# Seven buffers for the input tiles, and the row transform in four slices between them

## The chip, the cores and the metric

The kernel runs on one core of a Trainium2 chip. The metric is device time in microseconds (us), the median of several runs. The core has a matrix engine (TensorE, PE in the profile; its weight loads are PEld), two elementwise engines (VectorE, DVE, and ScalarE, ACT), a general engine (GpSimd, POOL) and a queue engine (SyncE, SP) that issues transfers. Each engine takes its own instructions strictly in order; they meet at semaphores. Transfers run on 16 DMA engines, whichever engine issued them. SBUF is the on-chip memory of 128 partitions, PSUM the memory that TensorE writes to, HBM the memory outside.

## What is computed

The input `x` has 8 batches of 32 channels of 256 x 256 points. Four layers follow each other, each of them `x + conv(groupnorm(x))`: a spectral convolution, a 5 x 5 convolution, a recurrence along the columns, and a mix of directional maxima. Only the first layer matters here:

```
x_ft   = rfft2(groupnorm(x))
out_lo = einsum('bixy,ioxy->boxy', x_ft[:, :, :32, :32],  w1)   # 32 x 32 lowest modes
out_hi = einsum('bixy,ioxy->boxy', x_ft[:, :, -32:, :32], w2)
x      = x + irfft2(out_ft) + bias
```

Only 64 x 32 of the modes are kept, so the forward transform is two small matrix products: one along the columns of an image (256 points to 32 complex modes), one along its rows (256 points to 64 complex modes). The normalisation is applied to the spectrum afterwards, with the mean and the sum of squares of each pair of channels.

## The kernel before

`forward_and_mix` makes the spectrum and multiplies it by the weights. The later functions (`inverse_and_conv`, `recurrence`, `maxima_and_mix`) are not touched, but the first of them shares SBUF with what is touched.

**Forward transform.** The work goes tile by tile: 8 batches (`b`) of 8 tiles (`n`) of 4 channels, 64 tiles in all. A tile `xa` is 1024 KB (8 KB in each partition), read from HBM by SP (L117). Its pool has four buffers (L103), so the loop keeps three loads ahead of the tile in work (L207, L211). A buffer can be loaded again when its three readers are done: the column matmuls on PE (L132), the squares of half of it on ACT (L141), and the squares of the other half on DVE (L142). The column transform lands in PSUM (`yp`, three buffers), and DVE turns it into `y` (L145). `y` holds a whole batch and has two buffers.

When the eight tiles of a batch are through, the row transform `over_rows` of that batch follows in one piece: 64 matmuls with 32-row operands (L158), two records each in the profile, into four banks of PSUM (`sp`). It stands after the column matmuls of the first tile of the next batch (L217). Right behind it in the same function DVE turns the result into `xb` (L166) and makes two small copies (L171, L172). `statistics` (L179 to L191) comes one tile later, `normalise` two tiles after that (L197, L198): it scales the spectrum, and sends a turned copy of it to `xf` by four transfers that POOL issues (L202).

**Order.** The order on each engine is the order of this code. No planner moves anything in these stages (`manual_schedule`), so what stands behind a waiting instruction on its engine waits too. On DVE the turn L166 stands ahead of the squares L142 of the next tile.

**Weights and mixing.** The weights are eight tiles `wt` of 2048 KB (16 KB in each partition), q = 0 to 7. The first two have buffers of their own in the pool `wp` and are loaded during the last batch, the first of them ahead of the last two input tiles (L212). The other pools of the forward transform are then given up, and a pool `wp2` with four buffers takes their place for q = 2 to 5; its first load (L243, issued at L99) waits until everything of the forward transform is done, the last `xf` transfers included. Tiles 6 and 7 reuse the buffers of 0 and 1 in `wp`. For each q there are 128 matmuls (L258, two records each), copies out of PSUM on ACT (L275) and DVE (L273), and two writes of 256 KB into the HBM tensor `smd` in rows of 128 bytes (L276), one issued by ACT and one by SP.

**What follows.** `inverse_and_conv` reads the spectrum `spec` back from `smd` (L337) and has six buffers for a second copy of the input, `xb<-in_xl_dram`, of 768 KB a load, issued by POOL (L367). These buffers lie in the same part of SBUF as the weight tiles of `wp2`. Their first load waits for the last reader of what was in this part; in the kernel before that is the mixing with q = 5.

Of the kernel before, what the change touches and what calls it, by code (L numbers as in the profile page):

```python
# [9 lines left out]
F32 = mybir.dt.float32  # L10
# [6 lines left out]
P = 128  # L17
B, C, H, W = 8, 32, 256, 256
NG = 16
KM = 32  # L20
# [57 lines left out]
def forward_and_mix(tc, k, d, smd, xmean):  # L78
# [4 lines left out]
    nc = tc.nc  # L83
    CH = 4
    NK = C // CH
    HB = H // 32
    KC = 4
    HW = float(H * W)
    with ExitStack() as ctx:
        one = ctx.enter_context(tc.tile_pool(name="m1", bufs=1))  # L90
        wp = ctx.enter_context(tc.tile_pool(name="mw", bufs=2))


        xf = one.tile([P, 2, B, KM, KM], F32, name="xf")
# [2 lines left out]
        def load_weights(q, wp):  # L97
            wts[q] = wp.tile([P, KM, KC, C], F32, name=f"wt_{q}", tag="wt")
            nc.sync.dma_start(out=wts[q].rearrange("p y j o -> p (y j o)"), in_=d["wm"][q])  # L99

        with ExitStack() as inner:
            fwd = inner.enter_context(tc.tile_pool(name="a1c", bufs=1))
            xp = inner.enter_context(tc.tile_pool(name="a1x", bufs=4))  # L103
            wk = inner.enter_context(tc.tile_pool(name="a1w", bufs=2))
            sm = inner.enter_context(tc.tile_pool(name="a1s", bufs=2))
            ps = inner.enter_context(tc.tile_pool(name="a1p", bufs=1, space=PSUM))
            fh = fwd.tile([P, 2, HB, P], F32, name="fh")
            nc.sync.dma_start(out=fh, in_=d["fh"])
            junk = [fwd.tile([P, 2, 2 * H], F32, name=f"junk_{i}") for i in range(2)]
            units = [(b, n) for b in range(B) for n in range(NK)]  # L110
            zero = fwd.tile([P, B], F32, name="zero")
            xs, ys, squares, turned = {}, {}, {}, {}

            def load(u):
                b, n = units[u]
                xs[u] = xp.tile([P, 2, CH, H], F32, name=f"xa_{u}", tag="xa")
                nc.sync.dma_start(out=xs[u].rearrange("p t c h -> p (t c h)"), in_=d["xt"][b, n])  # L117
# [28 lines left out]
                    ys[b][:, n].rearrange("p r t y -> p (r t y)"), yp.rearrange("p r h -> p (r h)")  # L146
                )

            def over_rows(b):


                sp = ps.tile([P, CH, 512], F32, name=f"sp_{b}", tag="sp")
                y = ys.pop(b)
                for ri in range(2):
                    for t in range(HB):
                        for i in range(CH):
                            r = slice(32 * i, 32 * i + 32)
                            nc.tensor.matmul(  # L158
                                sp[:, i, 0 : NK * KM].rearrange("p (n y) -> p n y", y=KM),
                                lhsT=fh[r, ri, t, :],  # L160
                                rhs=y[r, :, ri, t, :],
                                start=ri == 0 and t == 0,
                                stop=ri == 1 and t == HB - 1,
                            )
                xb = wk.tile([P, KM, KM], F32, name=f"xb_{b}", tag="xb")
                nc.vector.transpose(  # L166
                    xb.rearrange("p y x -> p (y x)"),
                    sp[:, :, 0 : NK * KM].rearrange("p i (n y) -> p y n i", y=KM),
                )
                ex = sm.tile([P, 4, NG, 2], F32, name=f"ex_{b}", tag="ex")  # L170
                nc.vector.tensor_copy(ex, squares.pop(b).unsqueeze(1).unsqueeze(3).to_broadcast([P, 4, NG, 2]))  # L171
                nc.vector.tensor_copy(zero[:, b : b + 1], xb[:, 0, 0:1])  # L172
                turned[b] = xb, ex

            def statistics(b):
# [14 lines left out]
                dc = xb[0:32, 0, 0:1]  # L190
                nc.vector.scalar_tensor_tensor(dc, st[0:32, 0:1], -HW, dc, ALU.mult, ALU.add)  # L191
                turned[b] = xb, rs
# [11 lines left out]
                        )  # L204

            with tc.manual_schedule(engines=None):
                for u in range(3):  # L207
                    load(u)
                for u, (b, n) in enumerate(units):
                    if u + 3 < len(units):  # L210
                        load(u + 3)  # L211
                    if b == B - 1 and n in (2, 5):  # L212
                        load_weights(n // 3, wp)
                    over_columns(u)
                    if b > 0:
                        if n == 0:
                            over_rows(b - 1)  # L217
                        elif n == 1:
                            statistics(b - 1)
                        elif n == 3:  # L220
                            normalise(b - 1)
                over_rows(B - 1)
                statistics(B - 1)
                normalise(B - 1)
                by_group = fwd.tile([P, B, NG], F32, name="by_group")
                nc.vector.tensor_tensor(
                    by_group,
                    k.sel.unsqueeze(1).to_broadcast([P, B, NG]),
                    zero.unsqueeze(2).to_broadcast([P, B, NG]),
                    ALU.mult,  # L230
                )
                xm = ps.tile([P, B, NG], F32, name="xm", tag="st")
                nc.tensor.matmul(xm, lhsT=k.ones, rhs=by_group, start=True, stop=True)
                nc.vector.tensor_copy(xmean, xm)

        wp2 = ctx.enter_context(tc.tile_pool(name="mw2", bufs=4))
        sp = ctx.enter_context(tc.tile_pool(name="ms", bufs=2))
        ps = ctx.enter_context(tc.tile_pool(name="mp", bufs=4, space=PSUM))
        NQ = KM // KC
        KY = KM // 2  # L240
        with tc.manual_schedule(engines=None):
            for q in range(2, 6):
                load_weights(q, wp2)  # L243
            for q in range(NQ):
                if 2 <= q < 4:
                    load_weights(q + 4, wp)
                wt = wts.pop(q)
                mps = [
                    [ps.tile([P, 2 * B, 2, KY], F32, name=f"mp_{q}_{s}_{h}", tag=f"mp{s}") for h in range(2)]
                    for s in range(2)  # L250
                ]


                for ky in range(KM):
                    for j in range(0, KC, 2):
                        for s in range(2):
                            r = slice(64 * s, 64 * s + 64)
                            nc.tensor.matmul(  # L258
                                mps[s][ky // KY][32 * j : 32 * j + 64, :, :, ky % KY],
                                lhsT=wt[r, ky, j : j + 2, :].rearrange("p j o -> p (j o)"),  # L260
                                rhs=xf[r, :, :, ky, KC * q + j : KC * q + j + 2].rearrange("p r b x -> p (r b) x"),
                                start=True,
                                stop=True,
                            )
                for s in range(2):
                    sm = sp.tile([P, B, 2, KM], F32, name=f"sm_{q}_{s}", tag=f"sm{s}")
                    for h in range(2):
                        for j in range(KC):
                            r = slice(32 * j, 32 * j + 32)
                            src = mps[s][h][r, :, j % 2].rearrange("p (r b) y -> p b r y", r=2)  # L270
                            dst = sm[r, :, :, h * KY : (h + 1) * KY]
                            if s:
                                nc.vector.tensor_copy(dst, src)  # L273
                            else:
                                nc.scalar.copy(dst, src)  # L275
                    (nc.scalar, nc.sync)[s].dma_start(  # L276
                        out=smd[:, :, s, KC * q : KC * (q + 1)].rearrange("b r j o y -> (j o) (b r) y"),
                        in_=sm.rearrange("p b r y -> p (b r) y"),
                    )


def inverse_and_conv(tc, k, d, smd, xmean, x2d, stb):
# [8 lines left out]
    QP = Q + 2  # L291
    HW = float(H * W)

# [5 lines left out]
    with ExitStack() as ctx:  # L299
# [26 lines left out]
        def by_pair(t):  # L326
            return t.rearrange("p (k c g) -> p k c g", c=2, g=G)

        def twice(t, n):
            return t.rearrange("p (k g) -> p k g", g=G).unsqueeze(2).to_broadcast([P, n, 2, G])  # L330
# [11 lines left out]
        def spectrum(b):  # L342
# [14 lines left out]
            nc.vector.tensor_tensor(by_pair(up), by_pair(bias), twice(m1, 4), ALU.subtract)  # L357
            nc.vector.scalar_tensor_tensor(t[0:1, :, 0, 0], up[0:1], HW, t[0:1, :, 0, 0], ALU.mult, ALU.add)
            for a in range(A):
# [703 lines left out]
```

## Time and profile before

| | |
|---|---|
| time, median of 3 runs | 3496.8 us (3491.6 to 3498.0) |
| span of the profiled run | 3489.2 us |
| forward transform: first tile in, last tile in | 14.0 us, 251.7 us |
| first matmul of the mixing, last one | 271.3 us, 353.6 us |
| first matmul of the inverse transform (L388) | 372.0 us |

The profile can be read as a page of sums, as tables of busy time by stretch, as a list of who waited for whom, as the chain of work that ended last, or as a list of instructions in order of time. In the tables of stretches each engine has its busy time and its number of instructions (x), and then come the granted TensorE clock (1.00 is full), the share of time in which the DMA engines were busy (it can exceed 1 a little) and the bytes they moved. In a list by time the first two columns are start and duration in us, and the bracket at the end tells how long the engine had been idle and what it had waited for; "issue" is idle time for which no wait is recorded. "SPq" and "ACTq" are the queues of transfers.

The stages of interest are the first 372 us of the 3489 us. The rest is the same code on the same data in both kernels.

### The profile page before, as it was taken

What the parts mean: (1) busy time and instruction counts of PE and PEld (TensorE: products, weight loads), DVE (VectorE), ACT (ScalarE), POOL (GpSimd) and SP (SyncE); (2) the same over time, 40 slices, a digit from 0 to 9 for tenths busy, and PEclk for the clock granted to TensorE, in tenths of its full rate; (3) what the DMA queues carried; (4) which work ended last, traced back from release to release, by engine and by line L of the source; (5) the groups of instructions that cost most, each with busy time, mean ns of one, the idle gap of its engine ahead of it and who ended that gap; (6) DMA issues with size and microseconds to landing.
All of it is one profiled execution on the core that took longest, in us unless ns stands there. A gap on an engine that the chain in (4) does not pass through costs nothing.

```text
span 3489.2 us, 114177 instructions
## 1 busy us (share of the span) xinstructions
PE 3125.8 (90%) x48474; PEld 1700.8 (49%) x48474; DVE 2590.4 (74%) x5178; ACT 1810.0 (52%) x4098; POOL 883.8 (25%) x1211
## 2 busy tenths in 40 slices
PE   6776599999999969999999999999999867777787
PEld 4546244444444446666666666666666523232332
DVE  5553255556555548888888888888888889999998
ACT  3322255655665547777677777776777512222222
POOL 0010011111111025444444444454444400000000
PEclk9985699999999979999999999999999979999898
DMA  8887467777777445555455555545554377777775
GB/s 309 285 293 237 98 179 184 189 184 186 198 173 198 101 125 143 136 134 143 126 131 141 146 124 147 131 129 133 144 126 123 83 286 309 307 301 293 305 306 235
DMA packets 533869, 655.78 MB, mean 188 GB/s; under 512 B 394992, under 2 KB 395888, under 8 KB 507632
## 3 DMA queue, kind: packets, MB, share of 16 engines
q1 hardware_dynamic: 492272, 499.58, 50.9%
q0 software_dynamic: 15360, 79.70, 6.8%
q10 hardware_dynamic: 25728, 69.21, 5.0%
q8 instruction: 381, 6.24, 0.7%
q14 instruction: 128, 1.05, 0.1%
HBM read 371.54 MB, written 272.63 MB: 185 GB/s over the span
## 4 chain that ended last, share of the span: by engine, by line
PE 63%; DVE 22%; issue 4%; DMA 1%; SPq 1%; ACT 1%; POOL 0%; DVEq 0%; ACTq 0%; POOLq 0%
PE r L686 9%; PE r L660 8%; PE vp L446 7%; PE vp L454 7%; PE z L686 6%; PE ni L686 6%; PE z L660 6%; PE ni L660 5%; DVE rv L885 5%; PE up L405 4%; DVE dq L898 2%; DVE uq L899 2%; PE tp L388 2%; PE mp L258 1%; DVE top L896 1%
## 5 line engine op out<-in xcount | busy, mean ns | idle before, releaser
L739 POOL TENSOR_TENSOR xw<-xw,hs 128x256 f32<-128x256 f32 x512 | 349.8, 683 | 661.9 <-DVE hs L738 620.4
L936 ACT ACTIVATE ot<-o,bres 128x512 f32<-128x512 f32 x256 | 155.1, 688 | 551.6 <-PE o L920 545.0
L735 POOL TENSOR_TENSOR a<-zm,xn 128x256 f32<-128x256 f32 x510 | 392.5, 770 | 154.0 <-ACT zm L732 140.2
L728 ACT ACTIVATE rs<-r,brz 128x256 f32<-128x256 f32 x510 | 239.4, 469 | 286.0 <-PE r L660 285.8
L471 ACT ACTIVATE junk<-x 128x128 f32<-128x128 f32 (+1 forms) x384 | 202.8, 528 | 329.6 <-DVE x L465 323.5
L686 PE MATMUL r<-hs,wmain 128*128 128x256 f32 x1020 | 357.4, 432 | 1.9 <-DVE hs L738 1.2
L413 DVE TENSOR_TENSOR x<-up,xb 128x512 f32<-128x512 f32 x288 | 185.5, 686 | 227.6 <-PE up L405 217.6
L660 PE MATMUL r<-xn,whh 32*32 32x256 f32 x4080 | 323.8, 386 | 29.5 <-ACT xn L653 29.5
L729 DVE SCALAR_TENSOR_TENSOR n<-nh,bhh,rs 128x256 f32<-128x256 f32 x510 | 245.7, 482 | 114.0 <-ACT rs L728 114.0
L733 ACT ACTIVATE n<-n,bih 128x256 f32<-128x256 f32 x510 | 259.2, 508 | 132.2 <-DVE n L730 132.2
L660 PE MATMUL r<-hs,wih 32*32 32x256 f32 x4080 | 323.3, 386 | 0.0
L465 DVE SCALAR_TENSOR_TENSOR x<-vp,r,x 128x128 f32<-128x128 f32 (+2 forms) x512 | 236.8, 514 | 110.1 <-PE vp L454 109.9
L660 PE MATMUL ni<-hs,wih 32*32 32x256 f32 x4080 | 311.6, 373 | 2.6 <-issue 2.6
L660 PE MATMUL nh<-xn,whh 32*32 32x256 f32 x4080 | 312.5, 375 | 0.8 <-issue 0.8
L660 PE MATMUL z<-xn,whh 32*32 32x256 f32 x4080 | 311.8, 374 | 0.0
L660 PE MATMUL z<-hs,wih 32*32 32x256 f32 x4080 | 310.9, 373 | 0.3 <-issue 0.3
L686 PE MATMUL z<-hs,wmain 128*128 128x256 f32 x1020 | 303.8, 379 | 0.0
L686 PE MATMUL ni<-hs,wmain 128*128 128x256 f32 x1020 | 303.4, 379 | 0.0
L446 PE MATMUL vp<-x,c_conv 128*128 128x256 f32 (+2 forms) x768 | 290.0, 512 | 2.0 <-DVE x L465 2.0
L763 DVE TENSOR_TENSOR fm<-xw,fm 128x512 f32<-128x512 f32 x255 | 289.7, 1136 | 1.4 <-POOL xw L739 0.8
L920 PE MATMUL o<-dn,wsc 32*32 32x512 f32 x1536 | 208.4, 790 | 78.1 <-DVE dn L901 73.2
L454 PE MATMUL vp<-x,c_conv 64*64 64x256 f32 (+2 forms) x1536 | 277.7, 492 | 0.0
(160 smaller groups left out, 6277.0 us busy)
## 6 DMA issues: line engine op xcount, KB each, us to landing
xb<-in_xl_dram POOLq DMA_DIRECT2D x96, 768.0 KB, 6.0
xa<-in_xt_dram SPq DMA_DIRECT2D x64, 1024.0 KB
xw<-x2d SPq DMA_DIRECT2D x32, 2048.0 KB
x3d<-xw SPq DMA_DIRECT2D x256, 256.0 KB
fwd<-fm SPq DMA_DIRECT2D x256, 256.0 KB
x<-x3d SPq DMA_DIRECT2D x32, 2048.0 KB
fw<-fwd SPq DMA_DIRECT2D x32, 2048.0 KB
out_dram<-ot ACTq DMA_DIRECT2D x64, 1024.0 KB
```

Source lines behind the costliest of these rows:

```text
L446: nc.tensor.matmul(vp, lhsT=k.conv[:, 0:P], rhs=pair_of(u, ch, g, lo, hi), start=True, stop=False)
L454: nc.tensor.matmul(vp[o], lhsT=k.conv[r, P : P + 64], rhs=pair_of(u, ch, g, lo, hi, q0, r), start=False, stop=True,)
L465: nc.vector.scalar_tensor_tensor(x, src, state[u]["r"][ch][:, g : g + 1], x, ALU.mult, ALU.add, accum_out=s1[:, 0, n, ch, g : g + 1])
L660: return nc.tensor.matmul(out[rows(j)], lhsT=lhsT, rhs=rhs[rows(i)], start=start, stop=stop)
L686: nc.tensor.matmul(psums[n, key], lhsT=wmain[:, gate, :], rhs=prev[:, :, 1 : 1 + Q], start=gate == N, stop=False)
L728: nc.scalar.activation(r, p["r"], AF.Sigmoid, bias=brz[:, 0:1])
L729: nc.vector.scalar_tensor_tensor(m, p["nh"], bhh[:, 2:3], r, ALU.add, ALU.mult)
L733: nc.scalar.activation(m, m, AF.Tanh, bias=bih[:, 2:3])
L735: nc.gpsimd.tensor_tensor(a, zm, cur, ALU.mult)
L739: nc.gpsimd.tensor_tensor(raw, raw, new, ALU.add)
L763: ins = nc.vector.tensor_tensor(t[:, :, wi], x, last, ALU.max)
L920: nc.tensor.matmul(pts[b2][i][32 * j : 32 * j + 32].rearrange("p (w q) -> p w q", q=Q), lhsT=wsc[q, b2, t, :], rhs=src[j][q, b2], start=first,
```

## The change

The input tiles get seven buffers instead of four, so that six loads run ahead. The row transform is cut into four slices of 16 matmuls, and one slice each follows the column matmuls of the tiles n = 0 to 3 of the next batch. The turn L166 with its two copies becomes a function of its own and comes after tile n = 4, the statistics after n = 5, the normalisation after n = 7: DVE is to meet a result that is ready. For the last batch, which has no next one, the row transform is done in two halves of columns: the half that belongs to tiles 0 to 3 after the column matmuls of tile 6, the other half after tile 7.

The three more input buffers need 24 KB in each partition. To make room, `wp` keeps one buffer, so only weight tile 0 is loaded during the forward transform (now after all input tiles have been issued), and tile 1 joins those that are loaded afterwards; `wp2` gets five buffers, and tiles 6 and 7 reuse buffers there: tile 6 that of tile 1, tile 7 that of tile 2.

```diff
+    AHEAD = 7
+    SLICES = 4
...
-        wp = ctx.enter_context(tc.tile_pool(name="mw", bufs=2))
+        wp = ctx.enter_context(tc.tile_pool(name="mw", bufs=1))
...
-            xp = inner.enter_context(tc.tile_pool(name="a1x", bufs=4))
+            xp = inner.enter_context(tc.tile_pool(name="a1x", bufs=AHEAD))
...
-            def over_rows(b):
+            def over_rows(b, i, lo=0, hi=NK):
...
+                steps = [(ri, t) for ri in range(2) for t in range(HB)]
+                size = len(steps) // SLICES
+                for ri, t in steps[i * size : (i + 1) * size]:
+                    for c in range(CH):
+                        r = slice(32 * c, 32 * c + 32)
+                        nc.tensor.matmul(
+                            sps[b][:, c, lo * KM : hi * KM].rearrange("p (n y) -> p n y", y=KM),
+                            lhsT=fh[r, ri, t, :],
+                            rhs=ys[b][r, lo:hi, ri, t, :],
...
+            def turn(b):
...
-                for u in range(3):
+                for u in range(AHEAD - 1):
                     load(u)
                 for u, (b, n) in enumerate(units):
-                    if u + 3 < len(units):
-                        load(u + 3)
-                    if b == B - 1 and n in (2, 5):
-                        load_weights(n // 3, wp)
+                    if u + AHEAD - 1 < len(units):
+                        load(u + AHEAD - 1)
+                    if b == B - 1 and n == 2:
+                        load_weights(0, wp)
                     over_columns(u)
                     if b > 0:
-                        if n == 0:
-                            over_rows(b - 1)
-                        elif n == 1:
+                        if n < SLICES:
+                            over_rows(b - 1, n)
+                        elif n == SLICES:
+                            turn(b - 1)
+                        elif n == SLICES + 1:
                             statistics(b - 1)
-                        elif n == 3:
+                        elif n == SLICES + 3:
                             normalise(b - 1)
-                over_rows(B - 1)
+                    if b == B - 1 and n == NK - 2:
+                        for i in range(SLICES):
+                            over_rows(b, i, 0, NK // 2)
+                for i in range(SLICES):
+                    over_rows(B - 1, i, NK // 2, NK)
+                turn(B - 1)
...
-        wp2 = ctx.enter_context(tc.tile_pool(name="mw2", bufs=4))
+        wp2 = ctx.enter_context(tc.tile_pool(name="mw2", bufs=5))
...
-            for q in range(2, 6):
+            for q in range(1, 6):
                 load_weights(q, wp2)
             for q in range(NQ):
                 if 2 <= q < 4:
-                    load_weights(q + 4, wp)
+                    load_weights(q + 4, wp2)
```

## The prediction

> **What bounds the kernel now.** The change touches the first 372 us alone, so I read that part. First the waits of the queue that issues the loads, from 36 to 251 us (us in total, times, longest):
>
> ```profile
> SPq L117 <- DVE junk L142: 150.4, 52, 10.5
> SPq L117 <- PE yp L132: 20.5, 14, 2.4
> ```
>
> The loads of x wait for a buffer, mostly for DVE to finish with the old tile, once as long as 10.5 us. Then the DMA by stretch, around the row transform of batch 0:
>
> ```profile
> 30.00:42.00 12.00, 10.45 (x176) 7.46 (x180) 5.71 (x10) 5.67 (x10) 0.00 (x0) 1.00 1.01 424
> ...
> 43.00:49.00 6.00, 6.00 (x101) 4.03 (x99) 3.72 (x12) 0.95 (x2) 0.00 (x0) 1.00 0.15 37
> 49.00:54.00 5.00, 4.69 (x88) 2.73 (x84) 5.00 (x10) 0.75 (x1) 2.01 (x2) 1.00 0.88 354
> 54.00:64.00 10.00, 4.96 (x86) 2.72 (x76) 6.52 (x12) 4.89 (x9) 1.70 (x4) 1.00 0.98 306
> ```
>
> Undisturbed, the DMA is full at 424 GB/s: a tile of 1.049 MB takes 2.47 us. From 43 to 49 us it is nearly empty (0.15 busy). Why, the lists of DVE and PE by time show:
>
> ```profile
> 36.94 0.72 DVE L145 STREAM_TRANSPOSE y<-yp 128x512 f32<-128x512 f32 x1 [0.66 <-PE yp L132]
> 45.18 1.25 DVE L166 STREAM_TRANSPOSE xb<-sp 128x1024 f32<-128x1024 f32 x1 [7.53 <-PE sp L158]
> ```
>
> ```profile
> 36.81 3.72 PE L158 MATMUL sp<-y,fh 32*128 32x256 f32 x60
> 40.98 4.15 PE L158 MATMUL sp<-y,fh 32*128 32x256 f32 x68 [0.45 <-issue]
> 45.06 1.93 PE L132 MATMUL yp<-xa,c_fw 128*32 128x256 f32 x32
> ```
>
> DVE stands 7.5 us before the turn L166, with the squares of the following tiles behind it. No buffer comes free, the three loads ahead run out, and the DMA stops. So the forward transform is bound by transfers, with a hole of about 6.3 us per batch. Check: 14.0 (first tile in) + 63 x 2.47 + seven times 4.1 (the `xf` transfers, below) + 5 (weight tile 0, ahead of the last two tiles) = 203; the last tile came at 251.7, which leaves 48.4 for seven holes, 6.9 each. It fits.
>
> The end of the stage and the mixing, from the lists by time and the chain that ended last:
>
> ```profile
> 255.83 7.19 PE L158 MATMUL sp<-y,fh 32*128 32x256 f32 x128 [0.83 <-DVE y L145]
> ...
> 272.25 6.92 PE L258 MATMUL mp<-xf,wt 64*64 64x32 f32 x281 [0.58 <-DMA xf<-xb]
> ```
>
> ```profile
> 334.62 0.56 POOL L367 DMA_DIRECT2D xb<-in_xl_dram  x1 [64.88 <-PE mp L258]
> ```
>
> ```profile
> 335.79 18.41 DMA smd<-sm
> ...
> 357.80 2.96 DMA smd<-sm
> ```
>
> From last tile to end of rows is 11.35 us, from there to the mixing 9.2. Near the end of the mixing POOL starts six loads for the next stage, and the `smd` writes, needed two rounds later, take 18.4 us instead of 3. The packets by queue from 342 to 350 us (packets, MB, share) show how (q0 the loads, q1 and q10 `smd`):
>
> ```profile
> q0 software_dynamic: 548, 2.98, 89.8%
> q1 hardware_dynamic: 665, 0.09, 6.8%
> q10 hardware_dynamic: 626, 0.08, 6.4%
> ```
>
> About one small packet per large one: some 83 per us on a queue, where one write has 2048.
>
> **What the Trainium skill says.** "DMA: Bandwidth & Descriptors", section "Queues, rings and completion order": each DMA engine goes round the queues that have work, packet by packet. The counts above agree. "Runtime: NRT & Kernel Launch", "Instruction fetch mechanics": instructions come in blocks of 256, fetched by DMA. The trace agrees: with the DMA full, the mixing matmuls come in groups of 127 or 128 records (with their weight loads 256 instructions) with gaps of 2.4 to 2.6 us; with it empty, gaps of 0.2. "TensorE: Matmul & The Clock Gate", "What's actually happening": after about 3.4 us of idleness the clock is halved. Here a tile's matmuls took 1.93 us, and 3.59 after waits of over 3 us at 66 us. The same page, "LDWEIGHTS (loading the stationary operand)": columns / 1.2 ns, 107 for 128 columns, whatever the rows; no row of before shows it apart.
>
> **The change, part by part.**
>
> *Seven buffers, slices, later turn.* At tile n = 4 the last slice has been done since before that tile's column matmuls, so L166 finds its result; its 1.6 us with the copies delay the next squares by no more, and six loads ahead are 6 x 2.47 = 14.8 us of stock. All holes go. What can take their place, per batch: DMA 8 x 2.47 + 4.1 = 23.9 us. The 4.1: from 54 to 64 us, with the `xf` transfers, queue 1 moved 2.52 MB instead of 4.24. PE: 8 x 1.93 + 7.2 + 0.4 (statistics) = 23.0, in blocks of 128 records of 7.2 us, longer than the 6.2 us in which the full DMA brings a block in the mixing. DVE: 8 x 1.75 (its pitch where it never waits, from 50.13 to 51.88 us) + 1.6 + 0.8 + 0.7 = 17.1. So the DMA stays the bound, at 97% of which PE is busy too. Six of the `xf` groups fall before the last tile (that of batch 6 now comes with tile 63), and weight tile 0 comes after it. Last tile in: 14.0 + 63 x 2.47 + 6 x 4.1 = 194. With so little room PE will fall behind at times; I add 3 us (a choice; bounds 0 and 14, the first rival). 197 instead of 251.7: **-54.7 us**.
>
> *The last batch in halves.* Each half is again 128 records, half as long. By the skill's price four loads of 107 ns on four row groups side by side give 27 ns a record, 3.4 us a half; at today's rate of 56 ns it would be 7.2. The first half delays the last tile's columns, as PE has only 2.5 us between two tiles. Best: 9.5 us after the last tile. With one fetch gap of 2.5 us in each half, as in the mixing under full DMA: up to 14.5. Before: 11.35. I take **0**, with -2 and +3 as ends. The chain from the turn to the mixing (9.2 us) stays; the `xf` transfers of batch 6 lie ahead of it, beside matmuls.
>
> *Weight tile 1 after the stage.* Five loads instead of four stand before the mixing's writes: 2.1 MB, 5 us more of full DMA. Tile 1 is there about 7 us after its issue, when the matmuls of q = 0 end. No matmul waits for it. But for 5 us longer PE runs at 6.2 us a group instead of 3.8: **+2 to +3**.
>
> *The next stage's loads.* Weight tile 7 now lies in `wp2`, where those six buffers will be. In the changed program their first load waits for the matmuls of q = 7, not q = 5. That takes the collision out of the last two rounds: two gaps of 2.4 become 0.2, **-4.4**. But it moves it to the last `smd` writes, on which the reading back of the spectrum waits. Call the last mixing matmul M. Before: last write landed at M + 7.1. After: copies end at M + 2, writes start at M + 2.6; the loads start at M + 2.4 (as at 334.4 to 336.8), and 4.7 MB at 395 GB/s take 12 us. At 83 packets per us, 980 of 2048 pass until M + 14.4, with some 400 more while the loads start up (a guess), and the rest in 1 us: M + 15.4, **+8.3**. If the writes slip through first, M + 5.5 and the readback (8192 small packets) meets the loads instead: about +4.
>
> Mixing and handover: 2.5 - 4.4 + 8.3 = +6.4. Sum: -54.7 + 0 + 6.4 = -48.3, or 3448.5. I say **3449**.
>
> **The rivals.**
> - *PE becomes the bound.* Before, PE was busy 24.4 us per batch, slow clock included; with a fetch gap of 0.4 twice, 25.3. Seven batches at 25.3 after the first put the last tile at 14 + 20 + 177 = 211: 3463. For: PE is within 1 us of the DMA, and idle waits bring the slow clock back. Against: most slow stretches followed the holes.
> - *The handover costs nothing,* the halves save their 2 us and PE keeps up: -57.7 - 2 + 2.5 - 4.4 + 4 = -58, 3439. For: reads and writes of `smd` are short when undisturbed (3 us). Against: the packet counts.
> - *Slower.* The holes are not a matter of buffers: some other wait (ACT or PE) releases the tiles as late as DVE did, and the handover's 6 us stays: 3503. Against: PE is the last to release in only 20.5 us of waits, and the squares on ACT kept pace while DVE stood.
>
> **How the numbers follow.** Main case 0.68, PE-bound 0.15, free handover 0.13, slower 0.04. The range 3435 to 3466 takes in the first three with their bounds. Faster by over 0.2% (7 us) 0.95, within it 0.01, slower 0.04.
>
> **What would show it.** Right: no stretch with an empty DMA between 15 and 195 us, the waits of L117 on DVE short, the last tile at about 197, the mixing starting at about 217, L367 released by the end of the mixing, and a `smd` wait of over 10 us right before the readback. Wrong: PE busy without a break and tiles waiting in their buffers (first rival); the readback starting 3 us after the last `smd` write was issued (second); L117 waiting as before (third).

## The result, and the profile after

| | before | changed |
|---|---|---|
| time, median of 4 runs each | 3494.2 us (3480.9 to 3498.0) | 3443.2 us (3441.8 to 3444.8) |
| ratio, 95% interval | | 0.9861 [0.9833, 0.9888] |
| span of the profiled run | 3489.2 us | 3441.9 us |
| last tile in | 251.7 us | 194.5 us |
| end of the last row transform | 263.0 us | 207.3 us |
| first matmul of the mixing | 271.3 us | 215.7 us |
| end of its last matmul | 353.6 us | 295.3 us |
| readback of the spectrum begins | 360.9 us | 313.6 us |
| first matmul of the inverse transform | 372.0 us | 324.75 us |

The kernel became faster by 51.0 us by the medians. The profiled runs differ by 47.3 us, and the whole of that lies ahead of the inverse transform: its first matmul (L388, now L402) comes 47.26 us earlier. The further working uses these two profiled runs, unless another is named. (The kernel before has one run more here than in its own table above.)

First the waits of the queue that issues the loads (L119, formerly L117), from 36 to 195 us:

```profile
SPq L119 <- DVE junk L144: 80.2, 49, 2.8
SPq L119 <- PE yp L134: 38.1, 25, 1.9
```

The queue still waits often, since it runs far ahead, but its longest wait for DVE is 2.8 us where it was 10.5. That is about the transfer of one tile, and six are in stock. The stretches around the row transform of batch 0, and one in the middle (PE, PEld, DVE, ACT and POOL busy, clock, DMA share, GB/s), show what that does to the transfers:

```profile
30.00:42.00 12.00, 10.90 (x188) 7.16 (x184) 8.19 (x14) 5.51 (x10) 0.00 (x0) 1.00 1.01 419
42.00:54.00 12.00, 11.65 (x203) 6.99 (x196) 6.09 (x13) 5.75 (x10) 0.00 (x0) 1.00 1.01 416
54.00:66.00 12.00, 11.87 (x200) 7.72 (x204) 11.25 (x24) 5.24 (x8) 3.71 (x5) 1.00 1.02 412
108.00:132.00 24.00, 23.52 (x405) 14.94 (x400) 17.52 (x36) 10.83 (x19) 4.05 (x7) 1.00 1.02 385
```

The DMA is full in each of them; the stretch with a share of 0.15 is gone. In the last row another thing is to be seen: PE is busy for 23.52 of 24 us. So two resources are at their limit at once. PE's list by time shows how the slices lie:

```profile
36.64 2.01 PE L161 MATMUL sp<-y,fh 32*128 32x256 f32 x32
38.58 1.93 PE L134 MATMUL yp<-xa,c_fw 128*32 128x256 f32 x32
40.44 2.01 PE L161 MATMUL sp<-y,fh 32*128 32x256 f32 x32
```

A slice of 2.0 us and a tile of 1.93 us take turns, where one block of 7.9 us stood between two tiles before. At the end of the stage:

```profile
195.06 1.93 PE L134 MATMUL yp<-xa,c_fw 128*32 128x256 f32 x32
196.93 3.85 PE L161 MATMUL sp<-y,fh 32*128 32x128 f32 x128
200.71 1.93 PE L134 MATMUL yp<-xa,c_fw 128*32 128x256 f32 x32
203.48 3.85 PE L161 MATMUL sp<-y,fh 32*128 32x128 f32 x128 [0.84 <-DVE y L147]
215.67 0.39 PE L272 MATMUL mp<-xf,wt 64*64 64x32 f32 x2 [2.66 <-DMA xf<-xb]
```

ACT takes up the last tile at 194.53, but only at 195.06 does PE begin with the columns of the tile before it. It is one tile behind when the input ends. The two halves of the row transform take 3.85 us each.

The rest is in the chain of work that ended last, and in POOL's list by time:

```profile
297.07 16.30 DMA smd<-sm
...
316.89 5.99 DMA spec<-smd
```

```profile
295.91 0.56 POOL L381 DMA_DIRECT2D xb<-in_xl_dram  x1 [81.73 <-PE mp L272]
```

The loads of the next stage (L381) are released by the end of the mixing, as the change of pools implies, and the last `smd` writes, begun at about 297, take 16.3 us. Before, a write of 18.4 us lay in the mixing, and the last one took 3.

### The profile page after: what moved, and what is told of

Its sections match the earlier page's. It is cut to its first block, busy times and chain, and to the rows that moved or that the text cites. A ratio compares the mean times of both kernels' runs of the same rounds, so it can differ in the third digit from the quotient of the medians.

```text
span 3441.9 us, 114429 instructions
## 1 busy us (share of the span) xinstructions
PE 3118.1 (91%) x48602; PEld 1690.7 (49%) x48602; DVE 2589.1 (75%) x5178; ACT 1808.5 (53%) x4098; POOL 883.6 (26%) x1211
## 4 chain that ended last, share of the span: by engine, by line
PE 65%; DVE 21%; issue 3%; DMA 2%; SPq 1%; ACT 1%; POOL 0%; DVEq 0%; POOLq 0%; ACTq 0%
PE r L700 9%; PE r L674 8%; PE vp L460 7%; PE vp L468 7%; PE z L700 6%; PE ni L700 6%; PE z L674 6%; PE ni L674 5%; DVE rv L899 5%; PE up L419 4%; DVE dq L912 2%; DVE uq L913 2%; PE tp L402 2%; PE mp L272 1%; DVE top L910 1%
```

## The experiments

Eleven kernels were run. Times are medians of 4 runs (20 for one kernel, which is said there), with the ratio to runs of the kernel before on the same chip; where the text says a single run, there is only the profiled one. "Last tile" is the time at which ACT takes it up.

### Which half of the change does it

**Buffers alone.** Seven buffers and the pools of weights as changed, but the rows in one piece and turned at once, as before:

```diff
-                        if n < SLICES:
-                            over_rows(b - 1, n)
-                        elif n == SLICES:
+                        if n == 0:
+                            for i in range(SLICES):
+                                over_rows(b - 1, i)
                             turn(b - 1)
-                        elif n == SLICES + 1:
+                        elif n == 1:
                             statistics(b - 1)
-                        elif n == SLICES + 3:
+                        elif n == 3:
                             normalise(b - 1)
```

(The last batch's rows are in one piece too.)

> The changed kernel with the row transform in one piece again, at the first tile of the next batch, with its turn right behind it, and whole for the last batch; the seven buffers and the pools of the weights stay. My theory: the hole is a matter of stock. DVE stands some 10 us per batch, six loads ahead are 14.8 us, so the DMA keeps running: last tile in at 195 to 200 (changed kernel: 194.5), time about 3446. Rival: the late turn and the slices do most of it, since the squares wait behind the turn just as long: last tile at 225 or later, time 3470 or more.

Measured: 3443.8 us (3442.8 to 3444.7), ratio 0.9869 [0.9852, 0.9886]; last tile at 197.28, inverse transform at 325.64. The waits of the loads from 36 to 190 us, and one stretch in the middle:

```profile
SPq L119 <- DVE junk L144: 109.9, 49, 9.9
```

```profile
108.00:132.00 24.00, 23.47 (x428) 16.89 (x424) 16.69 (x33) 11.39 (x19) 3.46 (x5) 1.00 1.02 387
```

DVE stands before the turn as long as ever, and a load waits 9.9 us for it, yet the DMA stays full: six loads ahead bridge it. What follows: the stock alone removes the hole. In the changed kernel slices and late turn add nothing that shows in the time (3443.8 against 3443.2, and 3447.1 when the changed kernel was measured again).

**Slices alone.** Slices, late turn and halves, but four buffers and the weights as in the kernel before:

```diff
-    AHEAD = 7
+    AHEAD = 4
...
-        wp = ctx.enter_context(tc.tile_pool(name="mw", bufs=1))
+        wp = ctx.enter_context(tc.tile_pool(name="mw", bufs=2))
...
-        wp2 = ctx.enter_context(tc.tile_pool(name="mw2", bufs=5))
+        wp2 = ctx.enter_context(tc.tile_pool(name="mw2", bufs=4))
```

(with tiles 0 and 1 loaded in the last batch, and 6 and 7 into `wp`, as before)

> The changed kernel with four buffers of x again and the weight pools of before; slices, late turn and halves stay. My theory: without the stock the loads follow PE through tiles 0 to 3 (two pieces of 1.9 us each per tile, 3.75 us) and the DMA through tiles 4 to 7, and the xf transfers add to it: 26 to 28 us per batch, last tile at about 222, time about 3465 with the handover of before. Rival: the slices alone are enough, 25 us per batch: last tile at 214 or earlier, 3457 or less. Other rival: four buffers keep the holes: over 240, 3485.

Measured: 3448.4 us (3444.7 to 3451.1), ratio 0.9885 [0.9864, 0.9906]. One stretch in the middle, and the arrival of the last tile at ACT:

```profile
84.00:108.00 24.00, 23.01 (x392) 14.54 (x388) 15.95 (x33) 10.24 (x17) 3.07 (x5) 1.00 1.02 371
```

```profile
208.90 1.06 ACT L143 ACTIVATE junk<-xa 128x1024 f32<-128x1024 f32 x1 [1.30 <-DMA xa<-in_xt_dram]
```

Three loads ahead are enough too, once no DVE wait is long: the first tiles of batches 3 and 7 come at 87.07 and 184.97, which is 24.5 us per batch, against 23.4 in the changed kernel (shown below). I had expected 26 to 28; the first rival of that expectation came. The last tile comes 14.4 us later than in the changed kernel, 5 us of that because weight tile 0 is loaded ahead of the last two tiles. But the inverse transform starts at 329.89, only 5.1 us later, and the time is 5.2 us longer. Some 9 us come back behind the last tile, where this kernel keeps the old pools and so the old handover. The two halves of the change are two cures of one hole; the second of them needs no memory.

### What bounds the forward transform now

Three kernels, a single run each. The first leaves out half of the row transform's matmuls:

```diff
-                steps = [(ri, t) for ri in range(2) for t in range(HB)]
+                steps = [(ri, t) for ri in range(2) for t in range(HB // 2)]
```

> The changed kernel with half of the row transform's matmuls left out (t below 4 of 8), so that the spectrum is not the right one; all transfers stay. It asks whether PE or the DMA sets the pace of 23 us per batch, with PE busy 98% and the DMA full. DMA the bound (the prediction): the last tile still comes at 194 to 196, PE now waits for tiles, and only the end of the stage gets some 4 us shorter. PE the bound: PE needs 3.6 us less per batch, the last tile comes at 186 or earlier.

The second leaves out the `xf` transfers of all batches but the last, with zeros in their place:

```diff
+        nc.gpsimd.memset(xf[:, 1], 0.0)
...
-                for s in range(2):
+                for s in range(2 if b == B - 1 else 0):
```

> The changed kernel with the turned copies into xf left out for all batches but the last (that half of xf holds zeros, so the spectrum's product is wrong); all matmuls stay. If the DMA alone set the pace, 4.1 us less of transfers per batch would bring the last tile to 175 or so. If PE, which is busy 98%, is as close as it looks, the pace stays at 23 us per batch and the last tile at 192 to 195, with loads waiting for buffers.

The third does both.

> The changed kernel with both left out: half of the row matmuls, and the xf copies of all batches but the last (the result is wrong on both counts). If the two are level bounds, neither alone moves the last tile much and both together do: 2.47 us a tile without a break, the last one at about 170. If one of them was the only bound, this run gives the same as the one that left it out.

The same stretch in the three, in this order, each followed by the arrival of the last tile at ACT:

```profile
108.00:132.00 24.00, 21.14 (x342) 13.07 (x340) 18.07 (x35) 11.17 (x18) 3.46 (x5) 1.00 1.02 386
...
194.41 1.06 ACT L143 ACTIVATE junk<-xa 128x1024 f32<-128x1024 f32 x1 [1.31 <-DMA xa<-in_xt_dram]
```

```profile
108.00:132.00 24.00, 23.52 (x404) 14.92 (x400) 17.52 (x36) 10.24 (x17) 2.05 (x2) 1.00 0.98 355
...
191.44 1.06 ACT L144 ACTIVATE junk<-xa 128x1024 f32<-128x1024 f32 x1 [0.49 <-DMA xa<-in_xt_dram]
```

```profile
108.00:132.00 24.00, 22.84 (x376) 13.23 (x376) 18.76 (x36) 11.53 (x21) 1.46 (x1) 1.00 1.01 419
...
177.21 1.06 ACT L144 ACTIVATE junk<-xa 128x1024 f32<-128x1024 f32 x1 [1.31 <-DMA xa<-in_xt_dram]
```

These marks count from the start of the run, and the first tile does not come at the same time in every run: at 13.88 us in the changed kernel's profile, at 16.00 in a second profile of it (below), at 15.75, 16.35 and 16.17 here. Counted from the first tile, the last one comes after 180.7 and 178.3 us in the changed kernel, and after 178.7, 175.1 and 161.0 us in these three. Less work for PE alone moves it not at all: the DMA holds it, at 386 GB/s. Fewer transfers alone move it by some 3 us: now PE holds it, and the DMA falls to 355 GB/s. Both together bring it 17 us earlier. So neither is the bound alone; they are level. The times were 3439.2, 3443.6 and 3422.5 us, beside 3492.5 for the kernel before.

The pace says the same. PE's list of the changed kernel has the statistics of batch 0 and of batch 6:

```profile
54.08 0.38 PE L186 MATMUL ms<-zero,c_msel 128*128 128x1 f32 x2 [0.43 <-DVE zero L179]
...
194.53 0.38 PE L186 MATMUL ms<-zero,c_msel 128*128 128x1 f32 x2 [0.43 <-DVE zero L179]
```

Six batches in 140.45 us are 23.4 us per batch, with one wait of 0.43 us in each. In the first of the three kernels, where the DMA alone sets the pace, the first tiles of batches 3 and 7 come at 81.07 and 174.44, which is 23.3 us per batch. In the third they come at 81.02 and 162.08: 20.3 us per batch, or 2.53 us a tile. What is left of 23.3 is an estimate for a group of `xf` transfers, 3.1 us. The prediction had 2.47 and 4.1. In the third kernel I had expected the last tile at 170; from 156 to 180 us its PE is busy for 23.52 of 24 us again, so that its last tiles wait for PE.

### The last batch in halves

The changed kernel with the last batch's rows in one piece after the last tile (a single run), and the changed kernel itself once more:

```diff
-                    if b == B - 1 and n == NK - 2:
-                        for i in range(SLICES):
-                            over_rows(b, i, 0, NK // 2)
                 for i in range(SLICES):
-                    over_rows(B - 1, i, NK // 2, NK)
+                    over_rows(B - 1, i)
```

> The changed kernel with the last batch's row transform in one piece after the last tile, not in two halves. By the prediction's step the halves are worth nothing, between 2 us saved and 3 lost: the rows end at 207 in both, the mixing starts at 215 to 217. If the halves save their time: rows end at 209 or later. If the first half held up the last tile: at 205 or earlier.

> The changed kernel itself, beside the others of this call: 3443 again, between 3440 and 3447.

The arrival of the first tile at ACT and the rows on PE, first with the rows in one piece, then in the changed kernel's second profile:

```profile
15.67 1.06 ACT L143 ACTIVATE junk<-xa 128x1024 f32<-128x1024 f32 x1 [13.64 <-DMA xa<-in_xt_dram]
...
202.28 7.19 PE L161 MATMUL sp<-y,fh 32*128 32x256 f32 x128 [1.77 <-DVE y L147]
```

```profile
16.00 1.06 ACT L143 ACTIVATE junk<-xa 128x1024 f32<-128x1024 f32 x1 [13.97 <-DMA xa<-in_xt_dram]
...
205.58 3.85 PE L161 MATMUL sp<-y,fh 32*128 32x128 f32 x128 [0.84 <-DVE y L147]
```

In one piece the rows end at 209.47, in the changed kernel at 207.33 and, in its second profile, at 209.43. These 2.1 us between two profiles of one program are those by which the first tile came later. Counted from the first tile, the rows of the changed kernel end after 193.45 and 193.43 us, and after 193.43 and 193.41 in the first two kernels of the next section, which have the same code up to there. In one piece they end after 193.80. So the halves are worth 0.4 us, which cannot be seen in a time: two halves of 3.85 us are 0.5 us more matmul than one piece of 7.19, and the wait for `y` before them is 0.84 us instead of 1.77. Times: 3444.8 us in one piece, 3447.1 (3444.0 to 3447.8), ratio 0.9872 [0.9858, 0.9887], for the changed kernel again.

### Where the rest of the gain went: the handover

The last tile comes 57.2 us earlier, but the inverse transform 47.3, and the medians gained 51.0 us and, measured again, 43.2. Two kernels try to get the difference back, and two more follow them up.

**The collision back in the mixing.** Weight tile 6 goes into tile 0's buffer, 1 and 7 share a pool of their own outside the part of SBUF that the next stage takes. The loads L381 then wait for the mixing with q = 5 again:

```diff
+        wp1 = ctx.enter_context(tc.tile_pool(name="mw1", bufs=1))
-        wp2 = ctx.enter_context(tc.tile_pool(name="mw2", bufs=5))
+        wp2 = ctx.enter_context(tc.tile_pool(name="mw2", bufs=4))
...
-                load_weights(q, wp2)
+                load_weights(q, wp1 if q == 1 else wp2)
...
-                    load_weights(q + 4, wp2)
+                    load_weights(q + 4, wp if q == 2 else wp1)
```

> The changed kernel with weight tiles 1, 6 and 7 out of the pool wp2: 6 in the buffer of tile 0, 1 and 7 in a pool of one buffer, so that the next stage's first load waits for q = 5 again. If the collision of these loads with the last smd writes costs the handover 11 us: the last write lands about 7 us after the last mixing matmul (changed kernel: 18), the mixing itself gets some 4 us longer, tile 1 comes a little earlier, the inverse transform starts 8 or 9 us earlier: 3434 to 3436. If the writes at the end are slow for another reason: last write still at 15 or more after the last matmul, 3443.

Measured: 3440.5 us (3436.2 to 3447.2), ratio 0.9861 [0.9841, 0.9882], so not the 3434 to 3436 that I had hoped for. Its chain that ended last, and PE at the start of the mixing:

```profile
215.79 8.96 DMA xf<-xb
...
288.69 17.97 DMA smd<-sm
...
310.26 2.95 DMA smd<-sm
```

```profile
219.78 0.39 PE L273 MATMUL mp<-xf,wt 64*64 64x32 f32 x2 [4.67 <-DMA xf<-xb]
```

The last `smd` write is short again, 2.95 us. But the write of 18 us is back in the mixing, which takes 86.6 us from first to last matmul where the changed kernel needs 79.6. And tile 1's load, which no longer waits for the forward transform to end, now runs beside the last `xf` transfers, and they take 8.96 us instead of 2.8. From the last mixing matmul to the inverse transform it is 18.6 us where the changed kernel needs 29.5, so 10.9 are gained, but 6.9 are lost in the mixing, and the mixing begins 2.1 us later, counted from the first tile. The inverse transform starts at 324.89 (changed kernel: 324.75 and, in its second profile, 325.85): the collision was moved, not removed. That tile 1's load makes the `xf` transfers long is read from this one profile; no kernel here takes it away alone.

**The loads after the readback.** The changed kernel, and ahead of the first load of the next stage one copy on POOL of a number of the spectrum into the load's buffer. The load has to follow that copy, and the copy has to follow the readback:

```diff
+                if u == 0 and ch == 0 and i == 0:
+                    nc.gpsimd.tensor_copy(t[:, 0, 0, 0:1], specs[0][:, 0, 0, 0:1])
```

> The changed kernel, with the next stage's loads held back until the spectrum has been read: GpSimd copies one number of it into the first buffer ahead of the first load. If the collision is the cause: last smd write 5 us after the last mixing matmul, readback and preparation 11 us, inverse transform at 312 instead of 324.7, and the loads land well before the first addition that needs them: about 3430. If it is not: 3443. If the loads then come too late for that addition: DVE waits for xb, and part of the 13 us is lost.

Measured: 3431.85 us (3430.1 to 3433.7), ratio 0.9835 [0.9818, 0.9852], faster than both kernels. Its chain, and then the list by time of POOL, PE and DVE:

```profile
298.53 4.21 DMA smd<-sm
...
306.15 6.05 DMA spec<-smd
```

```profile
313.33 3.26 POOL L383 DMA_DIRECT2D xb<-in_xl_dram  x6 [2.92 <-issue]
...
314.13 1.98 PE L404 MATMUL tp<-c_eh,spec 128*64 128x256 f32 x8 [3.33 <-DVE spec L372]
...
336.70 1.29 DVE L429 TENSOR_TENSOR x<-up,xb 128x512 f32<-128x512 f32 x2 [22.25 <-PE up L421]
```

The last write takes 4.2 us instead of 16.3, and the inverse transform starts at 314.13, 10.6 us earlier although the first tile came 2 us later. From the last mixing matmul to there it is 17.4 us instead of 29.5. The loads are issued at 313.33, 17 us later, and nobody misses them: the first that needs `xb`, the addition at 336.70, waits for PE alone. That shows the collision as the cause of the long write, and its price as some 12 us.

**The same edit on the kernel before.**

> The kernel before with one edit: the next stage's loads are held back until the spectrum has been read. If their collision with the smd writes cost the kernel before something too: the gaps of 2.4 us in the last two rounds of the mixing go, the wait of 18.4 us for smd goes, the inverse transform starts at 366 to 367 instead of 372.0: 3488 to 3490 beside 3494. If the collision cost nothing there, because it lay inside the mixing: no change.

Measured: 3487.4 us (20 runs) beside 3490.4 of the kernel before (23 runs), ratio 0.9991 [0.9985, 0.9998]. PE's list by time:

```profile
342.48 6.76 PE L258 MATMUL mp<-xf,wt 64*64 64x32 f32 x240 [0.16 <-issue]
...
366.89 1.98 PE L390 MATMUL tp<-c_eh,spec 128*64 128x256 f32 x8 [3.42 <-DVE spec L358]
```

The mixing takes 77.6 us from first to last matmul instead of 82.3, and the handover after it 17.7 instead of 18.4. So in the kernel before the collision cost 5.5 us between the first matmuls of the mixing and of the inverse transform (3.0 by the medians of the time), in the changed one some 12. The change doubled it. Compared with the loads held back in both, the forward part is worth 366.89 - 314.13 = 52.8 us.

**Five buffers, slices, the old pools of weights, loads held back.** If slices need little stock, five input buffers leave room for both early weight tiles:

```diff
-    AHEAD = 7
+    AHEAD = 5
...
-                    if b == B - 1 and n == 2:
-                        load_weights(0, wp)
+                    if b == B - 1 and n in (4, 5):
+                        load_weights(n - 4, wp)
```

(with `wp` of two buffers, `wp2` of four, and the copy on POOL)

> Slices and late turn with five buffers of x, the weight pools of the kernel before (tiles 0 and 1 loaded early, but both after the last tile of x), and the next stage's loads held back. Four loads ahead are 9.9 us of stock, and four buffers with slices already gave 24.3 us per batch: last tile at 195 to 198, mixing from about 217, with four weight loads instead of five ahead of the writes 2 to 3 us shorter than in the changed kernel, handover 17.5 us: inverse transform at 310 to 312, about 3428. If seven buffers are needed: last tile at 204 or later, 3436.

Measured: 3432.25 us (3424.6 to 3436.4), ratio 0.9829 [0.9812, 0.9847]; last tile at 199.15 (195 to 198 expected), inverse transform at 315.23. It is not better than the kernel with seven buffers and held loads (3431.85). From the first tile to the mixing it takes 204.3 us instead of 201.8, in the mixing 77.4 instead of 79.1: what the early tile 1 may gain, the forward transform loses.

## Why the prediction was right, point by point

The predicted 3449 is 5.8 us above the median; the likeliest case is the one that came, and its sum agrees with the profiled runs within about 1 us, -48.3 against -47.2. That closeness is in part luck: the terms missed by -2.5, +1.6, -0.8 and +2.8 us and cancelled.

| step | predicted | measured |
|---|---|---|
| last tile in | -54.7 | -57.2 |
| from there to the mixing | 0 (-2 to +3) | +1.6 |
| mixing, first to last matmul | +2.5 - 4.4 = -1.9 | -2.7 |
| last mixing matmul to inverse transform | +8.3 | +11.1 |
| sum | -48.3 | -47.2 |

**The forward transform.** The diagnosis held: the waits on DVE and the empty DMA went together, and the last tile came at 194.53, where the working gave 194. The 3 us that I added for PE falling behind did not show at the last tile. They belong to what follows: PE falls behind the tiles, and the end of the rows keeps its distance to the first tile within 0.04 us whether the last tile comes 178 or 181 us after the first. Two sizes in the working were off and cancelled in large part: a tile takes 2.53 us rather than 2.47, a group of `xf` transfers 3.1 rather than 4.1. The cause "DVE stands" was right, but either cure was enough, and the prediction treated them as one.

**"So the DMA stays the bound"** was half right. PE is as near to its limit: removing work from one of them gains some 3 us at most, from both 17. The sign that I had named for the first rival, PE busy without a break, is there but for one wait of 0.43 us per batch, and tiles do wait in their buffers. What the rival had wrong is its price: 25.3 us a batch with slow clock and fetch gaps. Measured were 23.4 us, at full clock. The slow stretches left with the holes: from 140 to 195 us the granted clock (third column from the end) was 0.88 in the kernel before, as the first line shows, and is 1.00 in the changed one, the second.

```profile
140.00:195.00 55.00, 43.03 (x664) 26.85 (x660) 33.04 (x65) 18.59 (x31) 6.92 (x10) 0.88 0.84 303
```

```profile
140.00:195.00 55.00, 53.62 (x908) 33.77 (x900) 38.25 (x74) 23.25 (x39) 6.92 (x10) 1.00 1.01 382
```

**The last batch in halves.** From the last tile to the mixing +1.6 us in the pair of profiles that I compare, but +3.8 in the second profile of the same kernel (194.32 to 217.73), so "0, with -2 and +3" was the right order. The last tile is a poor mark for this step, as PE works from its buffers: from the first tile to the mixing the two profiles agree, 201.8 and 201.7 us. The halves ran at 3.85 us for 128 records, 30 ns each. The Trainium skill, "TensorE: Matmul & The Clock Gate", section "LDWEIGHTS (loading the stationary operand)", had led me to an estimate of 27, and the trace is near it. But that does not show that the weight loads set this pace: half of the 56 ns at 256 columns would be 28. The prediction was wrong to say that no row of the kernel before shows these loads: its profile records them, with 185 ns each as a median where the estimate had 107, and it is 185 to 187 in the changed kernel too. These records overlap, so they do not give the pace either. No fetch gap fell in the halves here; in the kernel with five buffers one of 1.50 us did. What the prediction lacked is that PE is a tile behind when the input ends: it has no idle time there that the first half could fill, so that 0.4 us is all that the halves save.

**The mixing.** Right in sum. "No matmul waits for it", said of weight tile 1, was wrong, as PE's list by time in the changed kernel shows:

```profile
224.87 1.06 PE L272 MATMUL mp<-xf,wt 64*64 64x32 f32 x27 [2.35 <-DMA wt<-in_wm_dram]
227.04 3.64 PE L272 MATMUL mp<-xf,wt 64*64 64x32 f32 x128 [1.11 <-issue]
...
284.92 10.37 PE L272 MATMUL mp<-xf,wt 64*64 64x32 f32 x367 [0.46 <-issue]
```

The kernel before has a fetch gap at the same place, after its first 283 records:

```profile
282.70 3.64 PE L258 MATMUL mp<-xf,wt 64*64 64x32 f32 x128 [3.53 <-issue]
```

In the changed kernel the wait of 2.35 us lies 27 records ahead of that place, and the gap itself is then 1.11 us: together 3.46 us where one gap of 3.53 was, so the wait cost nothing. The last rounds run without the gaps of 2.4 us, as said (the last two are 0.37 and 0.46 us), and in the kernel before holding the loads back made the mixing 4.8 us shorter, near the 4.4 of the prediction.

**The handover.** The mechanism was right, the term mis-sized: +8.3 predicted, +11.1 measured. I had put the last write's end at the last mixing matmul + 15.4; it came at 313.37, that is + 18.1. The packets by queue (packets, MB, share), first from 299 to 302 us, then 302 to 311, then 311 to 314, show why:

```profile
q0 software_dynamic: 137, 0.74, 67.0%
q10 hardware_dynamic: 1499, 0.19, 40.6%
q1 hardware_dynamic: 16, 0.00, 0.4%
```

```profile
q0 software_dynamic: 643, 3.56, 94.5%
q1 hardware_dynamic: 641, 0.08, 5.8%
q10 hardware_dynamic: 511, 0.06, 4.6%
```

```profile
q1 hardware_dynamic: 1407, 0.18, 38.0%
q0 software_dynamic: 38, 0.14, 11.0%
```

In the middle stretch, packets of the loads (q0) and of the write that SP issued (q1) pass one to one, 643 to 641, as the Trainium skill, "DMA: Bandwidth & Descriptors", section "Queues, rings and completion order", says of queues with work. (The profile counts each row of 128 bytes as a packet; the page's packets hold several descriptors. What agrees is the turn-taking.) But I had both writes begin together and slip some 400 packets through while the loads start up. In fact one write (q10) had that opening and put 1499 of its 2048 through, while the other got 16. The late one then passed 71 packets a us for 9 us and had some 1400 left when the loads ended. The readback waits for the later of the two.

**The other rivals.** The handover was not free: the readback began 16.5 us after the last write was issued (297.07 to 313.55), not 3. That 3439 lies nearer to the first median, 3443.2, than my 3449 owes nothing to it; measured again, the median was 3447.1. The slower case failed at its first sign, the waits of the loads.

## What to carry to other kernels

When loads stall because the engine that has to release their buffers is held up by another wait, compare two cures before paying for both: a stock longer than the longest wait for it (here 14.8 us against 9.9), or an order in which that engine never stands for long (here no memory at all, and 5 us slower). Count what the memory for the stock takes from the neighbours: moving buffers between pools changes which transfer is released when, and here that gave 11 of 57 us back. Transfers in small rows that someone is waiting for should not run beside big loads that nobody needs yet; one tiny dependent copy ahead of the loads was worth some 12 us here. And when two profiles are compared, count from the same event in both, not from the start of the run.

## What was not expected of the hardware

- The first tile came at 13.88 us in one profile and at 16.00 in another of the same program, and with it the end of the rows moved from 207.33 to 209.43. Counted from the first tile, four profiles of this code agree within 0.04 us there.
- Not only small rows suffer beside big loads: the `xf` transfers took 8.96 us instead of 2.8 in the one profile in which a weight tile's load ran beside them.
- Of two equal writes that were issued 0.3 us apart, one got 1499 packets in 3 us and the other 16. Which of them is served first in such an opening, the traces do not say; that stays open.
